# A two-layer network on one core: the second layer's input projection cut into parts of 128 and 64 channels, and its first-column copies issued at another place

## The chip, the core and the metric

The kernel runs on one core of one Trainium2 chip. A core has five engines that work side by side and meet only through semaphores: TensorE (PE, with its weight loads as PEld) multiplies matrices into PSUM, VectorE (DVE), ScalarE (ACT) and GpSimd (POOL) work on elements, and SyncE (SP) issues most DMAs. Each engine takes its instructions in the order in which the program issues them. The metric is device time in microseconds (us).

## What is computed

Layer 0 is a convolutional block with four directional scans over images of 192 x 64 x 64, for a batch of 8. It is not touched by the change. Its output is read as 4096 tokens of 192 channels for each image, and layer 1 works on these. In short form, for one image:

```python
xs = layernorm(x.reshape(L, 192)) * g + b
def mamba(x):                              # twice: on xs, and on xs with its channels reversed
    xc, z = split(x @ in_w.T)              # 192 -> 384 + 384
    xc = silu(causal_conv4(xc) + conv_b)
    dt, B, C = split(xc @ x_w.T)           # 12, 16, 16
    dt = softplus(dt @ dt_w.T + dt_b)
    h[t] = exp(dt[t] * A) * h[t-1] + dt[t] * xc[t] * B[t]     # 384 channels x 16 states
    y = sum_n h * C + D * xc
    return (y * silu(z)) @ out_w.T
out = xs + mamba1(xs) + mamba2(flip(xs))
```

## The kernel before

All of it is float32. Layer 1 is `tile_mamba_kernel`. It takes the tokens in blocks of T = 512 (class `Tokens`, 64 blocks), and each block in two **passes** (class `Pass`, i = 0 and 1, one for each mamba), so there are 128 passes, and they follow each other in `passes`.

The 384 inner channels are three blocks c of 128 partitions. The 16 states of a channel block are taken in pairs, so a pass consists of 3 x 8 = 24 **groups** (class `Group`, `SLOTS` = 24), numbered n = 8c + g. In a group:

- `inputs` (L805) lets GpSimd write dt * x * B into the tile `hs`, but for its first column;
- `decays` (L810) lets ScalarE write exp(dt * A) into the PSUM tile `da` with two activations, and then copy two first columns into `hs` (L817). There are two buffers for `da` (pool `l1_psd`, `bufs=2`, four of the eight PSUM banks);
- `scan` (L819) is one VectorE scan over 2 x 512 elements. It writes over `da`, or, in the four groups of the list `FAR` (slots 0, 12, 15 and 20), into `hs`;
- `keep` (L824) lets ScalarE save the last column as the state;
- `weigh` (L827) multiplies by C, on VectorE, or on GpSimd in the four far groups;
- `sum` (L831) adds the result into the PSUM tile `yp` with two TensorE matmuls by the identity.

The order of the work is written out by hand. The loop at the end walks over n, the groups of all passes. In step n it issues the list `before[n]`, then `inputs` of group n+3, `scan` of n, sums of older groups, `weigh` and `keep` of n, `decays` of group n+2, and then the list `behind[n]`. Everything else of a pass is put into these two lists at a slot (`at(before, n, slot, ...)`). This is where the next pass is prepared: `enter` (a channel block of the input projection is copied from PSUM into `xr`, with its halo of three columns), `gate` (the same for `z`), `convolve` (four matmuls by diagonal weights), `silu`, `low_rank`, `spread` (DMAs that broadcast B and C), `step` (six activations for dt), `refine`, `head`, `project` and `add` (output projection of the pass before), and for a new block of tokens `load`, `stats`, `scale` and `turn` (transposes).

`in_proj` (L649) is the input projection of one block of 128 output channels: two matmuls of 96 rows each into one PSUM bank. All results of TensorE but `yp` share a tag `bank` with two buffers of one bank each. The buffer that a tile gets, and the semaphores, are assigned by the framework when the program is built; the order on each engine stays the one that is written.

## Time and profile before

| | us |
|---|---|
| timed, median of 3 runs (lowest to highest) | 17048.71 (17040.25 to 17053.79) |
| profiled execution | 17039.48 |
| its span, from the first to the last instruction | 17037.7 |
| first scan of layer 1 starts at | 6088.5 |
| last scan of layer 1 starts at | 17023.6 |

The mean granted TensorE clock is 0.961. A pass of layer 1 takes 85.5 us on the average (start of its first scan to that of the next pass), which is 3.56 us for a group. In the stretch from 7500 to 17038 us, which holds nothing but layer 1 and some 111 passes:

| engine | busy us of 9538 |
|---|---|
| VectorE | 8971 |
| TensorE matmul | 8829 |
| GpSimd | 9115 |
| ScalarE | 7188 |

A row of a group of instructions gives the line, the engine, the operation, the tile written and those read, shapes and count; behind the bar the busy time and the mean of one in ns; behind the next the idle time of the engine just before these instructions, with what ended it. A row of the timeline gives start, duration and the idle time before, in brackets. A float32 matmul stands as two records. Busy times of TensorE overlap, so its sum is no measure of its use.

### The profile page before, as it was taken

Reading aid. Unit: us, or ns where it says so; the run is one execution under the profiler, and the core shown is the slowest. Engines: PE = TensorE matmul, PEld = TensorE weight load, DVE = VectorE, ACT = ScalarE, POOL = GpSimd, SP = SyncE. Lnnn points to the kernel's source line nnn. Section 1 sums busy time; section 2 is a strip of 40 time slices with the busy share of each in tenths; the row PEclk is TensorE's granted clock in tenths of the full one; section 3 lists DMA queues with packets and bytes.
Section 4 is the critical chain, followed back from the end, with each engine's and each line's share of the span. In section 5 each row is a group of like instructions: output and inputs, shape, how many; then the busy total and the mean of one; then the engine's idle time right before and its main releaser. Section 6 shows DMA issues by size and latency. Waiting matters only on the chain.

```text
span 17037.7 us, 151026 instructions
## 1 busy us (share of the span) xinstructions
PE 15890.9 (93%) x42192; PEld 6469.8 (38%) x42192; DVE 15270.0 (90%) x14474; ACT 11931.5 (70%) x25451; POOL 15166.4 (89%) x9955
## 2 busy tenths in 40 slices
PE   8999999999999989999999999999999999999998
PEld 2333333333333334444444444444444444444443
DVE  8888888888887869999999999999999999999999
ACT  5656666565666667777777777777777777777776
POOL 7787878778787869999999999999999999999999
PEclk8999999999999989999999999999999999999999
DMA  0000000000000022222222222222222222222222
GB/s 13 10 6 15 1 15 1 15 10 6 15 1 14 1 97 104 105 104 105 104 105 104 105 104 105 104 105 104 105 104 105 104 105 104 103 106 102 106 100 89
DMA packets 656220, 1196.98 MB, mean 70 GB/s; under 512 B 307928, under 2 KB 374832, under 8 KB 653840
## 3 DMA queue, kind: packets, MB, share of 16 engines
q1 hardware_dynamic: 654976, 1187.03, 18.7%
q8 instruction: 335, 5.49, 0.1%
q14 instruction: 509, 4.17, 0.1%
q10 hardware_dynamic: 400, 0.29, 0.0%
HBM read 1128.44 MB, written 58.72 MB: 70 GB/s over the span
## 4 chain that ended last, share of the span: by engine, by line
DVE 28%; ACT 10%; issue 9%; POOL 8%; PE 8%; DMA 7%; SPq 0%; DVEq 0%; POOLq 0%; ACTq 0%
DVE da L822 19%; DMA c_sb<-bc 6%; POOL hs L808 5%; DVE hs L829 4%; ACT da L814 3%; DVE hs L822 3%; PE yp L834 2%; PE dbl_ps L695 2%; PE g L239 1%; POOL hs L829 1%; PE yp L331 1%; DVE z L760 1%; DMA b_sb<-bc 1%; PE q L275 1%; ACT xc L687 1%
## 5 line engine op out<-in xcount | busy, mean ns | idle before, releaser
L808 POOL TENSOR_TENSOR hs<-dtx,b_sb 128x1022 f32<-128x1022 f32 x3072 | 7140.5, 2352 | 53.5 <-DMA b_sb<-bc 24.4
L822 DVE TENSOR_TENSOR_SCAN da<-da,hs 128x1024 f32<-128x1024 f32 x2560 | 5851.9, 2286 | 494.1 <-ACT hs L817 462.6
L834 PE MATMUL yp<-hs,ident 128*128 128x512 f32 x12288 | 5756.0, 602 | 41.5 <-POOL hs L829 19.5
L814 ACT ACTIVATE da<-dt,a 128x512 f32<-128x512 f32 x6144 | 4246.7, 691 | 436.0 <-DVE hs L822 257.5
L834 PEld LDWEIGHTS yp<-hs,ident 128*128 128x128 f32 x12288 | 2307.7, 193 | 3055.9 <-issue 2699.6
L829 DVE TENSOR_TENSOR hs<-da,c_sb 128x1024 f32<-128x1024 f32 x2560 | 3129.5, 1222 | 89.2 <-DVE da L822 0.5
L239 PE MATMUL g<-xp,w_gate_sb 16*128 16x512 f32 x8640 | 1815.4, 658 | 60.4 <-ACT dx L312 51.6
L825 ACT COPY state<-da 128x2 f32<-128x2 f32 x2560 | 399.4, 156 | 1990.1 <-DVE hs L829 1981.2
L674 PE MATMUL pc<-xr,conv_diag 128*128 128x512 f32 x3072 | 1565.4, 639 | 159.0 <-ACT dt L720 140.5
L652 PE MATMUL pi<-xT,in_w 96*128 96x512 f32 x3072 | 1447.7, 597 | 91.7 <-ACT y L790 44.3
L265 DVE TENSOR_TENSOR q<-g,h 128x512 f32<-128x512 f32 x2016 | 1352.8, 685 | 116.4 <-PE g L239 71.4
L275 PE MATMUL q<-q,ident 128*128 128x512 f32 x2688 | 1336.3, 620 | 0.0
L285 ACT ACTIVATE rc<-g,eps 128x512 f32<-128x512 f32 x672 | 462.0, 688 | 1115.6 <-DVE g L280 1115.6
L315 POOL TENSOR_TENSOR dx<-dx,xc 128x512 f32<-128x512 f32 x768 | 1079.3, 1405 | 158.5 <-ACT dx L312 136.6
L822 DVE TENSOR_TENSOR_SCAN hs<-da,hs 128x1024 f32<-128x1024 f32 x512 | 1167.6, 2280 | 55.0 <-POOL hs L808 55.0
L829 POOL TENSOR_TENSOR hs<-hs,c_sb 128x1024 f32<-128x1024 f32 x512 | 1205.0, 2354 | 1.2 <-ACT state L825 1.2
L269 POOL TENSOR_TENSOR q<-q,q 128x512 f32<-128x512 f32 x672 | 852.5, 1269 | 198.7 <-DVE q L265 194.6
L239 PEld LDWEIGHTS g<-xp,w_gate_sb 16*128 16x128 f32 x8640 | 495.4, 188 | 1306.9 <-DVE q L265 392.0
L259 POOL TENSOR_TENSOR lam<-lam,xc 128x512 f32<-128x512 f32 x672 | 941.2, 1401 | 33.6 <-ACT lam L256 33.6
L674 PEld LDWEIGHTS pc<-xr,conv_diag 128*128 128x128 f32 x3072 | 583.7, 197 | 1019.8 <-issue 656.9
L280 DVE TENSOR_TENSOR g<-g,ab 128x512 f32<-128x512 f32 x1344 | 933.8, 695 | 22.8
L165 POOL TENSOR_TENSOR xc<-xc,side 128x504 f32<-128x504 f32 x384 | 450.1, 1172 | 559.6 <-DVE xc L160 301.7
(140 smaller groups left out, 23356.5 us busy)
## 6 DMA issues: line engine op xcount, KB each, us to landing
b_sb<-bc SPq DMA_DIRECT2D x1024, 512.0 KB, 9.0
c_sb<-bc SPq DMA_DIRECT2D x1024, 512.0 KB, 8.9
xin<-in_x_dram SPq DMA_DIRECT2D x64, 384.0 KB, 3.6
mid<-ot SPq DMA_DIRECT2D x16, 1536.0 KB, 8.4
xt<-mid SPq DMA_DIRECT2D x64, 384.0 KB, 10.0
out_dram<-y SPq DMA_DIRECT2D x64, 384.0 KB, 2.6
bc<-dbl SPq DMA_DIRECT2D x128, 64.0 KB, 1.6
b<-bc SPq DMA_DIRECT2D x128, 8.0 KB, 7.3
```

The source lines that it names most:

```text
L239: nc.tensor.matmul(dst, self.wg[r, at, self.d, :], flat(self.xp[r, self.j]), start=True, stop=True)
L259: nc.gpsimd.tensor_mul(self.lam if self.j else self.hc, self.lam, direction(self.xc, self.d, self.j))
L265: nc.vector.tensor_mul(self.q[i], rows(self.g[i]), self.h[:, :, i : i + HW])
L275: nc.tensor.matmul(self.sum, ident, flat(term), start=(i == 0), stop=(i == 1))
L315: nc.gpsimd.tensor_mul(self.dx, self.dx, direction(self.xc, self.d, self.j))
L652: nc.tensor.matmul(pi, self.m.in_w[:, i, c * P : (c + 1) * P], self.tokens.xT[:, i, :], start=(i == 0), stop=(i == 1))
L674: nc.tensor.matmul(pc, self.m.conv_w[:, c, t, :], self.xr[c][:, t : t + T], start=(t == 0), stop=(t == 3))
L808: nc.gpsimd.tensor_mul(self.hs[:, :, 1:], dtx, self.p.b_sb[self.g][:, :, 1:])
L814: nc.scalar.activation(self.da[:, n, :], self.p.dt[self.c], AF.Exp, scale=self.p.m.a[:, self.c, at : at + 1])
L822: nc.vector.tensor_tensor_scan(h, da, hs, 0.0, ALU.mult, ALU.add)
L829: engine.tensor_mul(self.hs, self.h, self.p.c_sb[self.g])
L834: nc.tensor.matmul(self.p.yp[self.c], ident, self.hs[:, n, :], start=False, stop=stop)
```

## The change

- `in_w` and the transposed tokens `xT` get 128 partitions and two parts: channels 0 to 127, and channels 128 to 191 twice, once on partitions 0 to 63 and once on 64 to 127. For that, `load` fetches the last 64 channels of each token a second time (a second DMA), `xt` has 256 columns, `stats` takes the first 192 of them, and `scale` and `turn` work on all 256.
- `in_proj` takes a pair of output blocks. It issues the two matmuls of 128 rows, each into its own bank, and then the two of 64 rows, one on the lower and one on the upper half of the rows.
- The pairs are (0, 2) at slot 0, (1, 3) at slot 11 and (4, 5) at slot 14; 3 to 5 are the blocks of `z`. So `enter` of block 1 goes from slot 8 to 11, `gate` of block 0 from 13 to 11, and `gate` of block 2 from 16 to 14.
- The second half of `project` goes from slot 10 to 8 and its `add` from 12 to 10, `store` from 13 to 11. The tile `y` has one buffer where it had two.
- The residual in `project` takes 128 and 64 columns where it took 96 and 96; the second with a matrix `twice` that holds 0.5 on two diagonals.
- The first-column copy leaves `decays` and becomes `begin`, which is issued ahead of `weigh` and `keep` of group n, where `decays` comes behind them.

```diff
         def load(self):
-            self.xt = p2.tile([P, self.slices, CM], F32, tag="xt", name=f"xt_{self.tag}")
-            nc.sync.dma_start(self.xt, self.rows(mid))
+            self.xt = p2.tile([P, self.slices, 2 * P], F32, tag="xt", name=f"xt_{self.tag}")
+            nc.sync.dma_start(self.xt[:, :, :CM], self.rows(mid))
+            nc.sync.dma_start(self.xt[:, :, CM:], self.rows(mid)[:, :, P:])
...
-        def in_proj(self, c):
-            pi = bank(f"pi_{self.tag}_{c}")
-            for i in range(2):
-                nc.tensor.matmul(
-                    pi, self.m.in_w[:, i, c * P : (c + 1) * P], self.tokens.xT[:, i, :], start=(i == 0), stop=(i == 1)
-                )
-            return pi
+        def in_proj(self, *outputs):
+
+            x, w = self.tokens.xT, self.m.in_w
+            pis = [bank(f"pi_{self.tag}_{c}") for c in outputs]
+            for pi, c in zip(pis, outputs):
+                nc.tensor.matmul(pi, w[:, 0, c * P : (c + 1) * P], x[:, 0, :], start=True, stop=False)
+            for pi, c, half in zip(pis, outputs, halves):
+                nc.tensor.matmul(pi, w[half, 1, c * P : (c + 1) * P], x[half, 1, :], start=False, stop=True)
+            self.pi.update(zip(outputs, pis))
...
-            nc.scalar.copy(xr[:, 3:], self.in_proj(c))
+            nc.scalar.copy(xr[:, 3:], self.pi[c])
...
-                t.y = p2.tile([P, t.slices, CM], F32, tag="y", name=f"y_{t.tag}")
+                t.y = p2.tile([P, t.slices, CM], F32, tag="y", bufs=1, name=f"y_{t.tag}")
...
+
+        def begin(self):
             nc.scalar.copy(self.hs[:, :, 0], self.p.first[self.c][:, self.g * NG : (self.g + 1) * NG])
...
-        for half, slot in enumerate((5, 10)):
+        for half, slot in enumerate((5, 8)):
             at(behind, n + 1, slot, p.project, half)
             at(before, n + 1, slot + 2, p.add, half)
         if p.i == 1:
-            at(behind, n + 1, 13, p.tokens.store)
+            at(behind, n + 1, 11, p.tokens.store)
...
-        for c, slot in enumerate((0, 8, 0)):
-            at(before, n - 1, slot, p.enter, c)
+        for slot, outputs in ((0, (0, 2)), (11, (1, NC)), (14, (NC + 1, NC + 2))):
+            at(before, n - 1, slot, p.in_proj, *outputs)
+            for c in outputs:
+                at(before, n - 1, slot, p.enter if c < NC else p.gate, c % NC)
...
-        for c, slot in enumerate((13, 14, 16)):
-            at(before, n - 1, slot, p.gate, c)
...
             if now and now.g == 0:
                 now.p.accumulate(now.c)
+            if n + 2 < len(groups):
+                groups[n + 2].begin()
             if now and not now.far:
                 now.weigh()
                 now.keep()
```

More of the change, by code (lines that the diff above doesn't have):

```diff
@@ L18 @@
 KM = 96
+KR = CM - P
 CI = 384
@@ L541 @@
     nc.gpsimd.memset(never, NEVER)
-    ln_sb = const.tile([KM, 2, 2], F32, name="ln_sb")
-    nc.sync.dma_start(ln_sb, ln.rearrange("g (k p) -> p g k", p=KM))
+    twice = const.tile([P, KR], F32, name="twice")
+    nc.vector.tensor_scalar_mul(twice, ident[:, :KR], 0.5)
+    nc.vector.scalar_tensor_tensor(twice, ident[:, KR:], 0.5, twice, ALU.mult, ALU.add)
+    halves = slice(0, KR), slice(KR, P)
+    ln_sb = const.tile([P, 2, 2], F32, name="ln_sb")
+    nc.sync.dma_start(ln_sb[:, :, 0], ln[:, :P].rearrange("g p -> p g"))
+    for half in halves:
+        nc.sync.dma_start(ln_sb[half, :, 1], ln[:, P:].rearrange("g p -> p g"))
     nc.vector.tensor_scalar_mul(ln_sb[:, 0, :], ln_sb[:, 0, :], -0.5)
@@ L552 @@
         m = Mamba()
-        m.in_w = const.tile([KM, 2, 2 * CI], F32, name=f"in_w{i}")
-        nc.sync.dma_start(m.in_w, in_w.rearrange("(k p) o -> p k o", p=KM))
+        m.in_w = const.tile([P, 2, 2 * CI], F32, name=f"in_w{i}")
+        nc.sync.dma_start(m.in_w[:, 0], in_w[:P])
+        for half in halves:
+            nc.sync.dma_start(m.in_w[half, 1], in_w[P:])
         taps = const.tile([P, NC, 4], F32, name=f"conv_w{i}")
@@ L601, in stats @@
                 st = p2.tile([P, 6], F32, tag="st", name=f"st_{self.tag}_{s}")
-                nc.vector.bn_stats(st, self.xt[:, s, :])
+                nc.vector.bn_stats(st, self.xt[:, s, :CM])
                 nc.vector.bn_aggr(self.mv[:, s, :], st)
@@ L627, in turn @@
             if i == 0:
-                self.xT = p2.tile([KM, 2, T], F32, tag="xT", name=f"xT_{self.tag}")
-            pt = bank(f"pt_{self.tag}_{i}", (KM, T))
+                self.xT = p2.tile([P, 2, T], F32, tag="xT", name=f"xT_{self.tag}")
+            pt = bank(f"pt_{self.tag}_{i}")
             for s in range(self.slices):
-                nc.tensor.transpose(pt[:, s * P : (s + 1) * P], self.xt[:, s, i * KM : (i + 1) * KM], ident)
+                nc.tensor.transpose(pt[:, s * P : (s + 1) * P], self.xt[:, s, i * P : (i + 1) * P], ident)
             nc.scalar.activation(
@@ L646, in __init__ @@
             self.xc = self.z = None
-            self.xr, self.pc, self.yp, self.first = {}, {}, [], {}
-        def in_proj(self, c):
-            pi = bank(f"pi_{self.tag}_{c}")
-            for i in range(2):
-                nc.tensor.matmul(
-                    pi, self.m.in_w[:, i, c * P : (c + 1) * P], self.tokens.xT[:, i, :], start=(i == 0), stop=(i == 1)
-                )
-            return pi
+            self.xr, self.pc, self.yp, self.first, self.pi = {}, {}, [], {}, {}
+        def in_proj(self, *outputs):
[6 more added lines that the diff above has]
+            self.pi.update(zip(outputs, pis))
         def enter(self, c):
@@ L682, in gate @@
                 self.z = p2.tile([P, NC, T], F32, tag="z", name=f"z_{self.tag}")
-            nc.scalar.copy(self.z[:, c, :], self.in_proj(NC + c))
+            nc.scalar.copy(self.z[:, c, :], self.pi[NC + c])
         def silu(self):
@@ L774, in project @@
                     )
-                for i in range(2 if self.i == 0 else 0):
-                    nc.tensor.matmul(
-                        self.po[:, s, i * KM : (i + 1) * KM],
-                        self.tokens.xT[:, i, at],
-                        ident[:KM, :KM],
-                        start=False,
-                        stop=(i == 1),
-                    )
+                for i, (to, ones) in enumerate(((slice(0, P), ident), (slice(P, CM), twice))):
+                    if self.i == 0:
+                        nc.tensor.matmul(
+                            self.po[:, s, to], self.tokens.xT[:, i, at], ones, start=False, stop=(i == 1)
+                        )
         def add(self, half):
@@ L896 @@
         for c in range(NC):
+            first.in_proj(c, NC + c)
             first.enter(c)
+            first.gate(c)
             first.convolve(c, range(4))
-            first.gate(c)
         first.silu()
@@ L913 @@
             if n < 2:
+                g.begin()
                 g.decays()
```

## The prediction

> **What bounds the kernel now.** The change touches layer 1 alone, 10.95 ms of the 17.04. The page's sums come first, then its costliest groups.

> ```profile
> PE 15890.9 (93%) x42192; PEld 6469.8 (38%) x42192; DVE 15270.0 (90%) x14474; ACT 11931.5 (70%) x25451; POOL 15166.4 (89%) x9955
> ...
> L822 DVE TENSOR_TENSOR_SCAN da<-da,hs 128x1024 f32<-128x1024 f32 x2560 | 5851.9, 2286 | 494.1 <-ACT hs L817 462.6
> ...
> L829 DVE TENSOR_TENSOR hs<-da,c_sb 128x1024 f32<-128x1024 f32 x2560 | 3129.5, 1222 | 89.2 <-DVE da L822 0.5
> ...
> L652 PE MATMUL pi<-xT,in_w 96*128 96x512 f32 x3072 | 1447.7, 597 | 91.7 <-ACT y L790 44.3
> ```

> Three engines look equally full, so the sums don't decide. VectorE's cadence does: a scan of 2.29 us and a product of 1.22 us, overlapping by 0.05, are 3.46 us for a group, and averaged over passes 10 to 125 of the trace VectorE idles over 0.1 us in three of the 24 slots only. In the stretch from 7500 to 17038 us it is idle for 9538 - 8971 = 567 us. The waits of that stretch say where:

> ```profile
> DVE da L822 <- ACT hs L817: 404.3, 208, 2.6
> ...
> PE dbl_ps L695 <- ACT xc L687: 273.2, 111, 3.5
> ...
> ACT da L814 <- DVE hs L822: 225.0, 111, 2.0
> ...
> DVE z L760 <- PE yp L834: 43.4, 53, 2.1
> ```

> With 111 passes in the stretch, that is about two waits of a scan for ScalarE in each pass, 3.6 us. VectorE waits for TensorE only 43 us in all. **So VectorE is the bound, ScalarE is what it waits for, and TensorE is behind neither**: where TensorE idles longest (L695) it waits for ScalarE. The timeline of pass 50 shows the two places, ScalarE first and then VectorE, slots 15 to 18:

> ```profile
> 10424.85 1.42 ACT L814 ACTIVATE da<-dt,a 128x512 f32<-128x512 f32 x2 [2.04 <-DVE hs L822]
> 10426.20 0.18 ACT L817 COPY hs<-first 128x2 f32<-128x2 f32 x1
> ...
> 10427.80 0.57 ACT L683 COPY z<-pi 128x512 f32<-128x512 f32 x1
> 10428.39 1.28 ACT L687 ACT_TABLE_LOAD   x1
> ...
> 10433.86 0.16 ACT L825 COPY state<-da 128x2 f32<-128x2 f32 x1
> 10434.05 1.42 ACT L814 ACTIVATE da<-dt,a 128x512 f32<-128x512 f32 x2
> ```
> ```profile
> 10422.53 2.28 DVE L822 TENSOR_TENSOR_SCAN hs<-da,hs 128x1024 f32<-128x1024 f32 x1
> 10426.41 2.30 DVE L822 TENSOR_TENSOR_SCAN da<-da,hs 128x1024 f32<-128x1024 f32 x1 [1.60 <-ACT hs L817]
> ...
> 10435.68 2.30 DVE L822 TENSOR_TENSOR_SCAN da<-da,hs 128x1024 f32<-128x1024 f32 x1 [2.25 <-ACT hs L817]
> ```

> The second stall (2.25 us) is the silu block: 5.46 us on ScalarE from the table load to the next `keep`, ahead of the exponentials of group 18. The first (1.60) is odd. The exponentials of group 16 wait until the far scan of group 15 ends, though two `da` buffers should let them follow the product of group 14. Only the buffer of group 15 comes free at that scan, so group 16 has its neighbour's buffer. The 111 waits of 2.0 us are this, once a pass. What is special about slot 14, from which these exponentials are issued: a `gate` copy stands on ScalarE ahead of them, and a far group follows. Ahead of the other far groups (slots 11, 19, 23) no copy stands there, and no such wait shows.

> **TensorE's saving.** Records of L652 follow at 0.43 us, two for a matmul; 12 matmuls a pass are 24 x 0.43 = 10.3 us. If two half-row matmuls take the time of one, 9 units remain, 7.7 us: 2.6 us a pass, 330 us in 128 passes. That they run together is seen in layer 0, whose gates lie in different groups of 32 rows (first row: weight loads; second: matmuls; four records, two gates):

> ```profile
> 3126.06 0.30 PEld L239 LDWEIGHTS g<-xp,w_gate_sb 16*128 16x128 f32 x4 [1.07 <-DVE g L280]
> 3126.06 1.13 PE L239 MATMUL g<-xp,w_gate_sb 16*128 16x512 f32 x4
> ```

> Four records in 1.13 us, against 1.88 for four of L652; the trace has the paired starts 7 ns apart. For 64 rows no row exists; the bounds are 0 and 330 us off TensorE's work, and I take 330. [...] I count the saving as nothing for the end; it lands in TensorE's idle time, such as L695's 273 us.

> **Gains on ScalarE.** The copy of z for block 2 leaves the queue ahead of the silu block: 10427.80 to 10428.39, 0.59 us earlier for group 18's scan. The first-column copy of group 16 no longer follows its exponentials but is done in ScalarE's 2 us of idle: 0.08. Those of groups 17 and 18 only change places within the full stretch. Together 0.67 us a pass; with 127 passes that prepare a successor, 85 us. In stretches where ScalarE idles anyway `begin` costs nothing; it can wait for GpSimd's `first` (L753), which ends 2.1, 3.0 to 4.1 and 3.3 us after scans 6, 14 and 22 start, about when `keep` was released by the product at 3.5, or ahead of a wait that lasts longer.

> **Losses on ScalarE.** Slot 11 now gets `enter` of block 1 (three copies, 0.80 us from start to next start) and a `gate` copy (0.59) between the exponentials of groups 12 and 13: 1.39 us. That is the fullest place outside silu, right behind the six activations of `step` (3.6 us):

> ```profile
> 10407.33 0.68 ACT L719 ACTIVATE e<-pd,vec_sb 128x512 f32<-128x512 f32 x1
> ...
> 10411.12 1.42 ACT L814 ACTIVATE da<-dt,a 128x512 f32<-128x512 f32 x2
> 10412.47 0.18 ACT L817 COPY hs<-first 128x2 f32<-128x2 f32 x1
> 10413.08 0.16 ACT L825 COPY state<-da 128x2 f32<-128x2 f32 x1 [0.43 <-DVE hs L829]
> 10413.27 1.42 ACT L814 ACTIVATE da<-dt,a 128x512 f32<-128x512 f32 x2
> ```

> Idle there: 0.43 us (0.50 in passes i = 1). Margin of group 13, from the end of its copy to VectorE's being free, over passes 10 to 125: 0.90 (i = 0) and 0.44 us (i = 1), plus 0.1 for the copy that is gone. For i = 0: 1.39 - 0.43 - 1.00, about nothing. For i = 1 the `y` copy (0.46) now also comes ahead of group 12: 1.39 + 0.46 - 0.50 - 0.54 = 0.8 us of stall, and up to 1.1 since the pair needs both banks: one is held until L720 reads it, the other until that `y` copy has, and the convolution behind it waits for `xr`. Mean over both kinds: 0.55.

> The other bound is **a second neighbour's buffer**. Slot 11 becomes what slot 14 is: copies that wait for TensorE ahead of the exponentials, and a far group (12) next. If group 13 gets group 12's buffer, its exponentials start when scan 12 ends, and scan 13, which follows at once because a far group has no product on VectorE, stalls by 1.42 + 0.03 = 1.45 us in both kinds of pass. It swallows the lateness above. The one row that there is, slot 14, speaks for it, and slot 11 has more copies, so I take 1.45. What else comes late there (`scale` with 64 more columns, some 0.06 us x 4) adds 0.05.

> **Edits at nothing.** `load`'s second DMA: SP issues one some 0.5 us, a pass ahead of its use (landing 10 us); no spread is waiting then. `store` two slots earlier follows its `add`. One buffer for `y`: rewritten some 20 slots (70 us) after the store, which lands in 2.6. `twice`, seven more loads at the start at 0.5 us, less 2.6 us of TensorE in the first pass: +1 us. Residual and transposes: TensorE alone.

> **Sum.** 1.45 + 0.05 - 0.67 = +0.83 us a pass, x 127 = +105; 17039.5 + 106 = 17145. The profiled execution lies 9 us below the median of the runs, within their scatter.

> **Rivals.** What this kernel's measurement can't tell from no change is 0.2%, 34 us.
> - Forecast, second buffer wait: 17145 (17110 to 17190 by itself), 0.45.
> - *No new buffer wait*, lateness alone: 0.55 - 0.67 = -0.12 us, 17024, no change. For it: on the chip ScalarE reaches group 13 before scan 12 ends. 0.18.
> - *Copies hidden*: the lateness is absorbed too, and 0.67 us stays, 16955. Against it: margins of 0.5 us at i = 1. 0.17.
> - *The old buffer wait goes* with the new order at slot 14: another 1.5 us a pass, 190 us, about 16840. Against it: slot 14 gets one copy more. 0.05.
> - *TensorE bounds after all*: 16710. Only its busy sum speaks for it. 0.03.
> - *Banks in series*: the pairs hold both banks until ScalarE has copied, TensorE falls back by some 5 us at slot 11, and the convolution's result (L678), queued on ScalarE ahead of group 15's exponentials, comes late as well; a second stall of 1.5 us: 17330. It decides once TensorE's lag at L678 exceeds the 1.3 to 1.7 us of group 15's margin. 0.12.

> The range leaves out the ends: 16940 to 17290. Faster 0.27 (hidden, old wait gone, TensorE, a piece of lateness alone), same 0.15, slower 0.58.

> **What would show it.** Right: a wait of VectorE for ScalarE of 1.4 to 1.5 us ahead of scan 13, with the exponentials released by the far scan (twice as many waits of L814 for a scan as before); at slot 18 a stall of about 1.65; TensorE's records of the halves starting together, and more TensorE idle. Wrong: no such wait at slot 13, or none at slot 16 either; or passes i = 1 alone longer, which is the lateness.

## The result and the profile after

| | before | after |
|---|---|---|
| timed, median of 4 runs (lowest to highest), us | 17051.25 (17040.25 to 17053.88) | 17251.08 (17249.35 to 17257.13) |
| ratio of the two, 95% interval | | 1.0119 [1.0105, 1.0133] |
| span of the profiled execution, us | 17037.7 | 17255.3 |
| mean granted TensorE clock | 0.961 | 0.945 |
| a pass of layer 1, mean of the 127 that another follows, us | 85.50 | 87.11 |

The change costs 200 us, where the forecast had 96 against the median then known. The lengthening of a pass, 1.60 us, makes 204 us over 127 passes, so all of it lies in the steady part of layer 1. (The two spans differ by 218 us; 14 of that came before the first scan of layer 1, which starts at 6102.2 us and in the runs below anywhere from 6088 to 6126.) From the page of the changed kernel, the sums of the engines and the rows of scan, product and input projection:

```profile
PE 15952.7 (92%) x42192; PEld 6325.8 (37%) x42192; DVE 15284.1 (89%) x14476; ACT 11912.6 (69%) x25451; POOL 15169.1 (88%) x9955
...
L835 DVE TENSOR_TENSOR_SCAN da<-da,hs 128x1024 f32<-128x1024 f32 x2560 | 5856.9, 2288 | 703.9 <-ACT da L825 697.5
...
L842 DVE TENSOR_TENSOR hs<-da,c_sb 128x1024 f32<-128x1024 f32 x2560 | 3129.3, 1222 | 88.8 <-DVE da L835 0.5
...
L666 PE MATMUL pi<-xT,in_w 128*128 128x512 f32 x1536 | 957.8, 733 | 499.1 <-ACT dt L734 252.9
```

VectorE's work is what it was: scan and product take the same time, its busy sum grew by 14 us (0.11 a pass). Its idle time ahead of a scan into `da` rose from 494 to 704 us, and ScalarE ends nearly all of it. New is the last row: TensorE, at the input projection's full-height matmuls, idles 499 us, and one record takes 733 ns on the average where it took 597. The waits of the stretch from 7500 to 17038 us, some 110 passes (us in total, times, longest):

```profile
DVE da L835 <- ACT da L825: 598.1, 326, 3.0
...
PE pi L666 <- ACT dt L734: 213.3, 108, 3.8
...
PE pi L666 <- DVE y L803: 170.2, 55, 3.8
ACT xc L692 <- PE pc L688: 159.7, 80, 3.9
ACT z L697 <- PE pi L668: 157.6, 109, 1.9
...
ACT xr L680 <- PE pi L668: 118.7, 55, 2.6
ACT da L825 <- DVE hs L835: 118.0, 79, 1.8
```

326 waits of a scan are three in each pass; before there were two. And three lines are new in kind: ScalarE waits for TensorE, 436 us in all, where the largest such wait before was 41 us. One of them (`xr`, 55 times) occurs in every second pass only.

The mean idle time of VectorE by slot, worked out from the trace over passes 10 to 125, tells the two kinds of pass apart (i = 0 / i = 1, us):

| ahead of the scan (or other work) of | before | after |
|---|---|---|
| slot 13 | none | 1.57 / 2.80 |
| slot 15 | none | 0 / 0.21 |
| slot 16 | 1.64 / 1.64 | 1.58 / 1.88 |
| slot 18 | 2.35 / 2.36 | 1.79 / 1.79 |
| slot 19 | 0.19 / 0.55 | 0.20 / 0 |
| whole pass | 4.84 / 5.20 | 5.77 / 7.26 |

So i = 0 is what was forecast, and i = 1 is not. Pass 51 (counted from 0, i = 1) starts at 10556.61. Its slots 10 to 13 in the timeline, TensorE, ScalarE and VectorE in this order:

```profile
10593.37 2.07 PE L666 MATMUL pi<-xT,in_w 128*128 128x512 f32 x2 [2.93 <-ACT dt L734]
10596.19 2.07 PE L666 MATMUL pi<-xT,in_w 128*128 128x512 f32 x2 [0.74 <-ACT y L801]
10598.19 1.96 PE L668 MATMUL pi<-xT,in_w 64*128 64x512 f32 x4
```
```profile
10595.68 0.46 ACT L801 COPY y<-po 128x384 f32<-128x384 f32 x1
...
10600.19 0.58 ACT L680 COPY xr<-pi 128x512 f32<-128x512 f32 x1 [2.34 <-PE pi L668]
...
10600.91 0.58 ACT L697 COPY z<-pi 128x512 f32<-128x512 f32 x1
...
10601.53 1.43 ACT L825 ACTIVATE da<-dt,a 128x512 f32<-128x512 f32 x2
...
10607.26 0.69 ACT L692 ACTIVATE xc<-pc,vec_sb 128x512 f32<-128x512 f32 x1 [2.78 <-PE pc L688]
```
```profile
10597.86 2.28 DVE L835 TENSOR_TENSOR_SCAN hs<-da,hs 128x1024 f32<-128x1024 f32 x1
10603.04 2.30 DVE L835 TENSOR_TENSOR_SCAN da<-da,hs 128x1024 f32<-128x1024 f32 x1 [2.91 <-ACT da L825]
```

Read it from the end. Scan 13 starts when its exponentials (10601.53) are done. These are not held by the far scan 12, which was over at 10600.14, but by the two copies in front of them on ScalarE, and the first of these waited 2.34 us for the half-row matmuls. TensorE had begun the pair late and did it in two pieces: the first matmul when L734 had read one bank, the second when the `y` copy (to 10596.14) had read the other. Each of its full-height matmuls took twice its usual time (two records in 2.07 us, for the 1.13 us of pass 121 further down). The granted clock of those 7.2 us says why; the windows of the changed kernel and, at the same place of its pass 51, of the kernel before (busy time and number of PE, PEld, DVE, ACT, POOL, then the clock, the DMA share and GB/s):

```profile
10593.00:10600.20 7.20, 6.08 (x9) 1.62 (x10) 7.14 (x5) 4.73 (x12) 6.96 (x6) 0.53 0.00 0
```
```profile
10492.10:10499.30 7.20, 6.21 (x16) 2.50 (x14) 7.20 (x6) 6.41 (x15) 6.92 (x6) 1.00 0.02 3
```

TensorE was given half its clock at the end of a gap of 2.93 us: 0.53 in the mean of this window, against 1.00.

### The profile page after: what moved, and what is told of

Read it like the earlier page. It is cut to its first block, busy times and chain, and to the rows that moved or that the text cites. A ratio compares the mean times of both kernels' runs of the same rounds, so it can differ in the third digit from the quotient of the medians.

```text
span 17255.3 us, 151478 instructions
## 1 busy us (share of the span) xinstructions
PE 15952.7 (92%) x42192; PEld 6325.8 (37%) x42192; DVE 15284.1 (89%) x14476; ACT 11912.6 (69%) x25451; POOL 15169.1 (88%) x9955
## 4 chain that ended last, share of the span: by engine, by line
DVE 22%; PE 14%; ACT 12%; issue 8%; DMA 7%; POOL 7%; SPq 0%; DVEq 0%; POOLq 0%; ACTq 0%
DVE da L835 16%; DMA c_sb<-bc 4%; POOL hs L819 4%; ACT da L825 4%; PE yp L847 4%; DVE hs L842 3%; DMA b_sb<-bc 2%; DVE hs L835 2%; PE pc L688 2%; PE pi L666 2%; PE pi L668 1%; PE g L240 1%; POOL hs L842 1%; PE yp L332 1%; PE q L276 1%
## 5 line engine op out<-in xcount | busy, mean ns | idle before, releaser
L847 PE MATMUL yp<-hs,ident 128*128 128x512 f32 x12288 | 5818.1, 611 | 95.2 <-POOL hs L842 59.5
L825 ACT ACTIVATE da<-dt,a 128x512 f32<-128x512 f32 x6144 | 4248.3, 691 | 313.6 <-DVE hs L835 138.5
L842 DVE TENSOR_TENSOR hs<-da,c_sb 128x1024 f32<-128x1024 f32 x2560 | 3129.3, 1222 | 88.8 <-DVE da L835 0.5
L688 PE MATMUL pc<-xr,conv_diag 128*128 128x512 f32 x3072 | 1496.4, 617 | 21.9 <-issue 16.6
L666 PE MATMUL pi<-xT,in_w 128*128 128x512 f32 x1536 | 957.8, 733 | 499.1 <-ACT dt L734 252.9
L161 DVE SCALAR_TENSOR_TENSOR xc<-pi,dw_sb,xc 128x504 f32<-128x504 f32 (+3 forms) x1152 | 834.0, 736 | 97.6 <-ACT xc L139 50.9
```

The lines of the kernel that those rows point to most:

```text
L666: nc.tensor.matmul(pi, w[:, 0, c * P : (c + 1) * P], x[:, 0, :], start=True, stop=False)
L688: nc.tensor.matmul(pc, self.m.conv_w[:, c, t, :], self.xr[c][:, t : t + T], start=(t == 0), stop=(t == 3))
L825: nc.scalar.activation(self.da[:, n, :], self.p.dt[self.c], AF.Exp, scale=self.p.m.a[:, self.c, at : at + 1])
L842: engine.tensor_mul(self.hs, self.h, self.p.c_sb[self.g])
L847: nc.tensor.matmul(self.p.yp[self.c], ident, self.hs[:, n, :], start=False, stop=stop)
```

## The experiments

Two theories stood: **the neighbour's buffer** (the forecast: the exponentials of a group wait for the far scan ahead of it, since the group was given that scan's buffer) and **the second bank** (the pair needs two PSUM banks at once, gets the second only after the `y` copy, and falls back). The kernels named a are edits of the changed kernel, those named b of the kernel before.

**Buffers alone.** Groups of even and odd number get their own tag for `da`, in the changed kernel and in the one before. In the programs as built this leaves no group in its predecessor's banks; else group 16 is there in the kernel before, and groups 13 and 16 in the changed one, in each of the 127 passes.

```diff
-            self.da = psd.tile([P, NG, T], F32, tag="da", name=f"da_{self.tag}")
+            self.da = psd.tile([P, NG, T], F32, tag=f"da{self.g % 2}", bufs=1, name=f"da_{self.tag}")
```

> The changed kernel, with one tag for each of the two da buffers, so that a group always gets the buffer of the group before the last and never its neighbour's. Theory A (neighbour's buffer at slots 13 and 16; in passes i = 1 also a late second bank and a halved TensorE clock): passes i = 0 lose both stalls, 1.57 us ahead of scan 13 and 1.58 ahead of scan 16, down to 0.1 each; passes i = 1 keep some 2.7 us ahead of scan 13, because there the exponentials start only after their copies. Mean gain 1.6 us a pass, about 17045 us. Rival B (the copies at slot 11 alone make ScalarE late): nothing changes, 17250.

Measured 17263.18 us, ratio to before 1.0129 [1.0114, 1.0144]: nothing gained in the sum. By kind of pass it is a gain and a loss: VectorE idles 4.53 / 8.60 us where it idled 5.77 / 7.26. The stall at 13 is gone in i = 0 (0.03) and longer in i = 1 (3.20), where slot 15 adds 1.03; at 16 it stays in both (2.0). Pass 51, ScalarE and then VectorE:

```profile
10600.80 0.59 ACT L680 COPY xr<-pi 128x512 f32<-128x512 f32 x1 [2.45 <-PE pi L668]
...
10608.89 0.69 ACT L692 ACTIVATE xc<-pc,vec_sb 128x512 f32<-128x512 f32 x1 [3.67 <-PE pc L688]
...
10613.38 1.07 ACT L697 COPY z<-pi 128x512 f32<-128x512 f32 x2 [1.58 <-PE pi L668]
```
```profile
10603.79 2.30 DVE L835 TENSOR_TENSOR_SCAN da<-da,hs 128x1024 f32<-128x1024 f32 x1 [3.16 <-ACT da L825]
...
10611.90 2.29 DVE L835 TENSOR_TENSOR_SCAN hs<-da,hs 128x1024 f32<-128x1024 f32 x1 [1.09 <-ACT da L825]
10616.14 2.30 DVE L835 TENSOR_TENSOR_SCAN da<-da,hs 128x1024 f32<-128x1024 f32 x1 [1.96 <-ACT da L825]
```

The buffers were free, and ScalarE still came late at slots 13, 15 and 16, each time behind TensorE. So a second lateness, TensorE's, stands behind the buffer wait. In i = 1 it has grown: the half clock begins in slot 11 in all 63 passes that prepare a successor, where it began in slot 10, and in pass 51 it takes in the sums behind the pair, four records in 3.00 us, where four take 1.88 us in pass 51 of the changed kernel (from 10607.06):

```profile
10600.70 3.00 PE L847 MATMUL yp<-hs,ident 128*128 128x512 f32 x4
```

> The kernel before, with one tag for each of the two da buffers. Theory A (the stall ahead of scan 16 is the neighbour's buffer): that stall of 1.60 us goes and the chain to scan 18 starts 1.5 us earlier, 127 x 1.5 = 190 us, about 16860 us. Rival B (ScalarE is late there anyway): 17050.

Measured 16851.5 us, ratio 0.9884 [0.9868, 0.9901]. In the kernel before, where TensorE isn't late, the same edit is worth 194 us, as foreseen. Pass 50: the exponentials of group 16 (10360.08) now run beside the far scan 15, and scan 16 follows with no wait:

```profile
10359.88 0.16 ACT L825 COPY state<-da 128x2 f32<-128x2 f32 x1 [0.78 <-DVE hs L829]
10360.08 1.42 ACT L814 ACTIVATE da<-dt,a 128x512 f32<-128x512 f32 x2
```
```profile
10359.77 2.28 DVE L822 TENSOR_TENSOR_SCAN hs<-da,hs 128x1024 f32<-128x1024 f32 x1
10361.96 2.27 DVE L822 TENSOR_TENSOR_SCAN da<-da,hs 128x1024 f32<-128x1024 f32 x1
```

**The second bank alone.** The second half of `project` is issued at slot 6 in place of 8 (its `add` at 8), so that its bank has been read long before slot 11; each half has its own `po`.

```diff
-        for half, slot in enumerate((5, 8)):
+        for half, slot in enumerate((5, 6)):
...
-            self.po = bank(f"po_{self.tag}_{half}", (P, 2, CM))
+            self.po[half] = bank(f"po_{self.tag}_{half}", (P, 2, CM))
```

> The changed kernel with the second half of project at slot 6 and its add at slot 8 (8 and 10 in the change; each half keeps its own PSUM tile), the pair still at slot 11. So the y copy stands no longer between L720 and the second bank. Theory A: in passes i = 1 both matmuls of 128 rows start when L720 has read its bank, about 2.7 us earlier; the stall ahead of scan 13 falls from 2.80 to the 1.5 of the neighbour's buffer, in passes i = 0 it stays at 1.57; 0.7 to 1.0 us a pass, 17120 to 17160 us. Rival (TensorE's clock alone, which its idle stretch halves still): 17230 to 17250.

Measured 17154.15 us, 1.0067 [1.0051, 1.0084]: 97 us gained on the changed kernel by the medians (89 by the two ratios), and what is left is the forecast's 17145 but for 9 us. The stall at slot 13 is 1.57 / 1.58, the same in both kinds of pass. Pass 51, the pair on TensorE and scan 13:

```profile
10544.78 1.02 PE L666 MATMUL pi<-xT,in_w 128*128 128x512 f32 x2
10546.24 1.12 PE L666 MATMUL pi<-xT,in_w 128*128 128x512 f32 x2 [0.43 <-ACT dt L734]
10547.30 1.13 PE L668 MATMUL pi<-xT,in_w 64*128 64x512 f32 x4
```
```profile
10554.54 2.30 DVE L835 TENSOR_TENSOR_SCAN da<-da,hs 128x1024 f32<-128x1024 f32 x1 [1.54 <-ACT da L825]
```

From the second matmul's start to the end of the halves it is 2.19 us; in the changed kernel it was 3.96, at half clock.

> As a_early_add, and with one tag for each of the two da buffers, which alone brought nothing. Theory A (two causes at slot 13, each of which hides the other): now the stall goes, ahead of scan 13 to at most 0.4 us, ahead of scan 16 to at most 0.5; about 16850 us. Rival (TensorE comes late at slot 14 whatever frees the bank): stalls of 1.5 to 2 us ahead of scan 16 stay, 17000 us.

Measured 17041.92 us, 1.0000 [0.9991, 1.0010]. With the bank free, the two tags gain 112 us where without that they gained nothing in the sum: what they are worth depends on TensorE's lateness. But it isn't 16850. In passes i = 0 there are now stalls of 1.01 and 2.03 us at slots 15 and 16, and pass 50 shows the bank as their start:

```profile
10423.91 1.02 PE L666 MATMUL pi<-xT,in_w 128*128 128x512 f32 x2
10430.66 2.08 PE L666 MATMUL pi<-xT,in_w 128*128 128x512 f32 x2 [5.73 <-ACT dt L734]
```

The first matmul ran early, into the bank that `add` had left; the second waited 5.73 us for `step` to read the other bank, and took 2.08 us for 1.02, at half clock.

**Clock and order.** *Sums first*: the two `sum` calls are issued ahead of the list `before[n]`, so that TensorE has work in front of the pair. *Warm*: three matmuls by a matrix of zeros, added into `yp`, go ahead of the pair at slot 11.

```diff
+            for by, far in ((3, False), (4, True)):
+                if g := earlier(n, by, far):
+                    g.sum()
             for part, args in before[n]:
...
+        def warm(self):
+            for _ in range(3):
+                nc.tensor.matmul(self.yp[1], zeros, self.xc[:, 1, :], start=False, stop=False)
...
+        at(before, n - 1, 11, passes[n - 1].warm)
```

> The changed kernel, with the sums of older groups issued ahead of the list before[n], so that TensorE has 1.7 us of work in its idle stretch ahead of the pair at slot 11. Theory A (that stretch of 3 us halves the clock, and the pair takes 4 us where it should take 2): the stall ahead of scan 13 in passes i = 1 falls from 2.80 to about 1.5, mean gain 0.8 us a pass, 17150 us, with few half-clock stretches at slots 10 and 11. Rival (the wait for the second PSUM bank alone): the bank comes free at the same time, 17240 to 17250.

Measured 17441.61 us, 1.0231 [1.0216, 1.0247]. The aim was met at slot 11 (stall 1.57 / 2.24), but the pair at slot 14 now stands behind two sums, and the copies of z wait for it as long as 3.6 us; ScalarE's waits of this run, in the same stretch, have 345 us where the changed kernel has 158:

```profile
ACT z L697 <- PE pi L668: 345.4, 107, 3.6
```

Slot 16 stalls by 2.71 / 3.00. The miss shows how little room TensorE has there: two sums of 1.9 us each, put ahead of a pair, come out at VectorE.

> The changed kernel with three matmuls by a matrix of zeros, added into yp, ahead of the pair at slot 11, so that TensorE's idle stretch there is filled by 2.6 us and nothing is reordered. Theory A (the idle stretch halves the clock): the pair takes some 2 us from the second bank's release where it took 4, the stall ahead of scan 13 in passes i = 1 falls from 2.80 to about 1.5, and the waits of ScalarE for TensorE at L692 and L697 shrink; 0.8 to 1.2 us a pass, 17100 to 17150 us. Rival (only the wait for the second bank counts): 17250, or more by what the added matmuls delay.

Measured 17224.74 us, 1.0103 [1.0088, 1.0118]: 26 us gained of the 100 or more expected. In i = 1 the stall at 13 fell from 2.80 to 2.05, with half clock in 23 of the 63 passes that prepare a successor in place of 58; but i = 0 got 0.44 us more at slot 19, and the added matmuls take TensorE's time themselves.

How much of this is the clock's, the passes of one kernel tell. In the changed kernel, passes 119 and 121 (both i = 1) have the same pauses ahead of the pair, and its second matmul begins 5.78 us after the start of scan 10 in both. The clock was halved in the first of them alone. The pair and scan 13, pass 119 and then pass 121, where the exponentials of group 13 stand between:

```profile
16509.77 1.13 PE L666 MATMUL pi<-xT,in_w 128*128 128x512 f32 x2 [1.26 <-ACT dt L734]
16512.59 2.08 PE L666 MATMUL pi<-xT,in_w 128*128 128x512 f32 x2 [1.69 <-ACT y L801]
16514.59 2.08 PE L668 MATMUL pi<-xT,in_w 64*128 64x512 f32 x4
16519.55 2.30 DVE L835 TENSOR_TENSOR_SCAN da<-da,hs 128x1024 f32<-128x1024 f32 x1 [3.02 <-ACT da L825]
```
```profile
16684.69 1.12 PE L666 MATMUL pi<-xT,in_w 128*128 128x512 f32 x2 [1.26 <-ACT dt L734]
16687.51 1.13 PE L666 MATMUL pi<-xT,in_w 128*128 128x512 f32 x2 [1.69 <-ACT y L801]
16688.57 1.13 PE L668 MATMUL pi<-xT,in_w 64*128 64x512 f32 x4
16691.49 1.42 ACT L825 ACTIVATE da<-dt,a 128x512 f32<-128x512 f32 x2 [0.32 <-DVE hs L835]
16693.00 2.30 DVE L835 TENSOR_TENSOR_SCAN da<-da,hs 128x1024 f32<-128x1024 f32 x1 [1.54 <-ACT da L825]
```

With the second bank just as late, but TensorE at full clock, ScalarE reaches group 13 with 0.32 us to spare, and what is left is the buffer's stall. The other passes i = 1 agree (mean stall ahead of scan 13 in us, by the clock during the pair):

| kernel | at half clock | at full clock |
|---|---|---|
| changed | 2.91 (58 passes) | 1.57 (5) |
| sums first | 3.05 (28) | 1.58 (35) |
| warm | 2.68 (23) | 1.67 (40) |

So the stall beyond the buffer's needs both, the late bank and the halved clock. The early `add` took away both: in that run a stretch at half clock begins in slots 9 to 11 in 7 of the passes i = 1. In the changed kernel the passes i = 1 at half clock are 1.8 us longer than those at full clock (86.55 and 84.71); over 58 passes that is some 105 us, an estimate, since it rests on five passes at full clock. It fits the 26 us of the warm run: there the difference is 1.4 us, and 35 passes fewer at half clock, less 0.44 us at slot 19 in 64 passes, make 20.

**The pair elsewhere.** Slot 9 in place of 11 for (1, 3), ahead of `step`, with `project` at slot 6. In the first two of these runs the second half of the output projection is added twice and the first left out, which leaves the amount of work as it is; the third has a `po` for each half and adds both.

```diff
-        for slot, outputs in ((0, (0, 2)), (11, (1, NC)), (14, (NC + 1, NC + 2))):
+        for slot, outputs in ((0, (0, 2)), (9, (1, NC)), (14, (NC + 1, NC + 2))):
```

> The changed kernel with the pair (1, 3), its enter and its gate at slot 9 instead of 11, and the second half of project at slot 6 instead of 8, so that both banks are free, ScalarE has 1.7 us of idle there, and no far group follows. Theory A: the stall ahead of scan 13 goes (1.57 and 2.80 us), the one ahead of scan 16 stays at 1.5 to 1.6, the one ahead of scan 18 at 1.7; 0.67 us a pass less than the kernel before, about 16965 us. Rival (the pairs of half-row matmuls, or the added columns, cost time wherever they stand): 17150 to 17250.

> As a_pair9, and with one tag for each of the two da buffers. Theory A: the stall ahead of scan 16 goes as well, another 1.5 us a pass, 16775 us. If TensorE's lateness lies underneath, as it did in the changed kernel with that edit: no gain over a_pair9, 16965.

> The changed kernel with the pair (1, 3) at slot 9, the second half of project at slot 6 and each half with its own PSUM tile, so that the first half is added as it should be (in a_pair9 the second half was added twice). Theory A: as a_pair9, no stall ahead of scan 13, 17046 us; with the gate copy gone from slot 16 down to 16980. Rival (the change is slow wherever the pair stands): 17150.

Measured 17046.08 us (1.0000 [0.9991, 1.0008]), 16864.6 (0.9893 [0.9878, 0.9908]) and 17040.12 (0.9998 [0.9988, 1.0007]); the first two are 81 and 90 us above what was expected. At slot 9 no stall is left at slot 13, in either kind of pass, and group 13 is no longer in its neighbour's buffer: the whole loss of the change hangs on slot 11. What remains of the change then gains nothing. Of the 0.57 us saved at slot 18 in the third run, some is paid at slot 19 (0.48 / 1.25), where VectorE waits for a sum of TensorE (`z <- yp`). Its longest rows of waits in that run (the second was 43.4 us in 53 waits in the kernel before):

```profile
DVE da L835 <- ACT da L825: 356.0, 222, 2.0
DVE z L774 <- PE yp L847: 96.7, 91, 2.1
```

**Parts of the change in the kernel before.** *Slots*: `enter`, `gate`, `project` and `store` at the slots of the change, with 96-row matmuls as before. *First column*: `begin` alone.

```diff
-        for half, slot in enumerate((5, 10)):
+        for half, slot in enumerate((5, 8)):
...
-        for c, slot in enumerate((0, 8, 0)):
+        for c, slot in enumerate((0, 11, 0)):
...
-        for c, slot in enumerate((13, 14, 16)):
+        for c, slot in enumerate((11, 14, 14)):
```

> The kernel before, with enter, gate, the second half of project and store at the changed slots, but with in_proj as it was: single output blocks, two matmuls of 96 rows. Theory A (the slots bring the neighbour's buffer at slot 13, the pair that holds back block 1 until both banks are free brings the rest): a stall of 1.5 us ahead of scan 13 in both kinds of pass, less 0.59 us at slot 18, about 17150 us, 100 less than the changed kernel. Rival (it is all in the slots): 17250.

Measured 17210.44 us, 1.0097 [1.0080, 1.0114]: 159 of the 200 us, between the two expectations. The slots carry most of the loss, with stalls of 1.49 / 1.81 at 13. That the pairs make it worse is seen in i = 1 alone, by 1 us at slot 13, where they need both banks before anything can be copied. This hangs on the clock too: the matmuls at slot 11 were at half clock in 29 of 63 passes here, with a stall of 2.1 us, against 58 and 2.9 with the pairs; at full clock both kernels stall by 1.5 to 1.6.

> The kernel before, with the first-column copies alone moved as in the change. Theory A: 0.08 to 0.1 us at the stall of slot 16 and nothing elsewhere, some 10 us, 17040 us. Rival (ScalarE, in order, now waits for GpSimd's first columns ahead of keep and the exponentials): slower by up to 0.5 us a pass, 17110 us.

Measured 17043.69 us, 1.0000 [0.9991, 1.0008]. The first-column copies cost and bring nothing that can be measured.

**A version better than both.** The kernel before with two tags for `da`, `begin`, and the last `gate` at slot 15.

```diff
-        for c, slot in enumerate((13, 14, 16)):
+        for c, slot in enumerate((13, 14, 15)):
```

> The kernel before with one tag for each of the two da buffers, the gate copy of block 2 at slot 15 instead of 16 (ScalarE idles 0.47 us there once the buffers alternate), and the first-column copies moved as in the change; single output blocks as before. Theory A: 0.5 to 0.6 us a pass less than with the two tags alone at the stall of scan 18, 16775 to 16790 us. Rival (the z copy is hidden anyway): 16850.

Measured 16822.53 us, 0.9870 [0.9855, 0.9885]: 221 us less than before, 429 less than the changed kernel, though 32 to 47 short of what was expected. The stall at slot 18 fell by 0.36 us, not 0.5. One wait of a scan for ScalarE is left for each pass, that of the silu block; beside it the waits for GpSimd's `hs` have grown, from 0.9 us:

```profile
DVE da L824 <- ACT da L814: 239.6, 111, 3.1
DVE da L824 <- POOL hs L808: 31.5, 47, 0.9
```

## Why the prediction was right in its sign and wrong in its size

The terms of the sum, us a pass, as the mean of both kinds of pass:

| term | forecast | measured |
|---|---|---|
| slot 13 | +1.45 | +2.19 |
| slots 15 and 16, forecast: first-column copy | -0.08 | +0.20 |
| slot 18, z's copy | -0.59 | -0.57 |
| slot 19 | 0 | -0.27 |
| forecast: `scale`; measured: VectorE's own work, rest | +0.05 | +0.05 |
| sum | +0.83 | +1.60 |

**The step that failed** is the pace of the pair in the term for slot 13, in passes i = 1. The prediction put 1.45 us into both kinds of pass and said of the buffer wait: "It swallows the lateness above." The lateness itself it had at 0.8 us, "up to 1.1 since the pair needs both banks". At full clock that holds: the stall is 1.57 us, and the exponentials of group 13 wait 0.32 us for the far scan. But the working has no term for TensorE's clock; it was put at nothing, without a reason. In place of this, the clock was halved in 58 of the 63 passes that prepare a successor. There the `y` copy ends (10596.14 in pass 51), the second matmul and both halves can run only after it and take 4 us for 2.2, then come two copies, and the exponentials of group 13 start 1.4 us after the far scan has set their buffer free: 2.91 us in these passes, 2.80 in the mean. Freeing the bank early, which also kept the clock up, brought i = 1 down to 1.58, and 97 us is the size of the two together; by the passes at full clock, the halved clock is needed for about all of it. That this run came to within 9 us of the forecast is in part luck: slot 13 takes 0.12 us more than was said, and slot 19, of which nothing was said, gives 0.20.

**The neighbour's buffer** was right: 1.57 us in i = 0 against 1.45, ended by the far scan, and the buffer assignment names group 13. The old one at slot 16 stayed, as said. So was the lateness of "about nothing" for i = 0: with the two tags the stall at 13 is 0.03 there. That this wait is worth what it looks like only where nothing else is late was not said: 194 us in the kernel before, nothing in the sum in the changed one, 112 us in the changed one with the bank free.

**The gain at slot 18** was right in place and near in size. Slot 19's change, 0.27 to the good, wasn't foreseen.

**TensorE "behind neither"** held for the kernel before and not for the one after. Its saving was said to land in idle time such as the 273 us ahead of `dbl_ps`; that wait is 109 us now. That the saving is worth nothing at the end was an estimate; the copies of the input projection out of PSUM (L680, L697) stayed at six a pass, 579 and 585 ns each where they took 575 and 579. The idle time went to slots 10 and 11, ahead of the pair, from which ScalarE waits for TensorE by 436 us. The half-row matmuls do run together (four records in 1.13 us, for 1.88 of four at full height), but the pair costs 2.88 us in line with nothing waiting (10608.77 to 10611.65 in pass 51, slot 14), not the 2.58 that the prediction's units make.

**The rival "Banks in series"** had the mechanism: both banks held, the convolution's result late (L692 waits 2.78 us in pass 51), a second stall behind it. It had the size wrong in the other direction, 1.5 us in every pass against the 0.20 above; slot 15 stalls in passes i = 1 at half clock alone (0.23 us, and none in the five at full clock). It is TensorE's lateness, though, and not the buffer, that keeps the changed kernel with two tags from gaining.

**Edits at nothing** can't have been dear: with the pair at slot 9 the kernel has all of them, and its time is that of before, the 0.57 us at slot 18 against 0.50 at slot 19. None was tried by itself but `begin`, which is nothing.

## What to carry to other kernels

A step that needs two buffers at once starts when the later of them is free: write down for both who reads them last and when, and follow the engine that waits through to the next one, at the speed that the trace shows for it there (here 2.07 us for 1.13 after a pause of 2.93). A wait lies hidden under one that ends later: the late bank cost nothing under the buffer's wait until the halved clock made it the longer of the two. So an edit shows its worth only beside the other waits (the two tags: 194, 0 and 112 us); try it where the other wait is absent too, and sort the passes of one run by what differs between them before you trust a mean. And before work is moved into a gap, look at which buffer the program as built gives to the group behind it, since the order of issue decided it here (group 13 had its neighbour's with the pair at slot 11, and not at slot 9).

## What the runs showed of the hardware

TensorE's clock was halved after short pauses, and not each time. In pass 51 of the changed kernel it fell at 10593.09, 2.65 us into the pause of 2.93. Of two passes with the same pauses, 1.26 us and 1.69 with a matmul at full speed between, it fell in pass 119 and stayed up in pass 121. The windows of both follow: the 3.41 us before the fall in pass 119, with TensorE busy for 1.25, and the 6.83 at half clock behind it, then the two stretches of 3.41 in pass 121, counted on from the last change of the clock, between which the same pauses were split, with 2.08 and 1.78 (behind its bounds and its length, a row begins with TensorE's busy time and records; the third number from the end is the clock):

```profile
16508.39:16511.80 3.41, 1.25 (x3) 0.30 (x2) 3.31 (x3) 3.35 (x7) 3.41 (x2) 1.00 0.01 2
16511.80:16518.63 6.83, 6.04 (x9) 2.00 (x10) 4.74 (x4) 4.28 (x13) 6.52 (x6) 0.50 0.01 2
16682.47:16685.88 3.41, 2.08 (x5) 0.43 (x3) 3.31 (x3) 3.35 (x7) 3.41 (x3) 1.00 0.00 0
16685.88:16689.29 3.41, 1.78 (x6) 0.60 (x6) 3.41 (x4) 3.20 (x8) 3.33 (x3) 1.00 0.00 0
```

Over the passes of the changed kernel, a stretch at half clock begins in slots 9 to 11 in 122 of 128; with the slots alone in 81, and in the kernel before, where TensorE does the second half of `project` there, in 33. The stretches that begin at slot 10 take 2.92 us of the clock a pass. It was no loss by itself where TensorE wasn't waited for: in passes i = 0 such a stretch begins in all 64, and their stall at slot 13 is the buffer's 1.57 us.
